# A decoder layer on one core: when the next sequence's first block may start, for the first two sequences

## The chip, the core and the metric

One of the eight cores of a Trainium2 chip runs the kernel. The metric is device time in microseconds (us), the median of several executions. All arrays are float32.

## What is computed

The layer takes 16 sequences of 512 tokens and 256 channels, and 64 context tokens of 128 channels for each. It has three blocks, and after each comes a layer norm of the input plus the block's result:

```python
x = layernorm(x + attn(x))      # gated long convolution, output projection, gated MLP
x = layernorm(x + xattn(x, ctx))
x = layernorm(x + ffn(x))       # low-rank: x@U1@V1 + b1, gelu, @U2@V2 + b2

# attn: z = rmsnorm(u)@in_proj.T, short causal conv, split in x2, x1, v
y   = (long_conv(x1*v) + x1*v*D_skip) * x2        # 16 poles per channel
y   = y@out_proj.T + u
mlp = gelu(zm@l1.T) * (zm@l2.T) @ l3.T            # zm = rmsnorm(y), 672 wide
return y + mlp

# xattn, 16 heads of 16:
y = softmax(causal(q@k.T))@v + softmax(qc@kc.T)@vc
return y@Wp + bp
```

Sequences are independent of each other in all of it.

## The kernel before

The kernel has two parts, each with a plan of its own. The front part goes over all 16 sequences and writes the long convolution (`yconv`) and the gates (`gates`) to DRAM. The second part, from line 990 on, goes through the sequences one after the other: `first_block(b)` (gate, output projection L1148, RMS norm, MLP L1173 to L1225, layer norm), `attention(b)` and `ffn(b)`. The change is in the second part.

The order of the work is not that of the code. Each step is recorded with `plan.op(engines, cost, fn, prio, ...)`. Dependencies come from the buffers that a step reads and writes (`r`, `w`) and from `after`. `Plan.schedule` (line 103) then plays the steps through with the given costs: at each moment a free engine takes, of the steps whose dependencies are done and whose buffers can be had, the one with the lowest priority number. On PE, `change` (line 95) adds a penalty or a bonus for leaving or keeping a tiling of the array. The result is one fixed order of instructions on each engine, in which each engine then runs on the chip. Priorities are built from the sequence: 1000 for each, so `first_block` of sequence b has (b-2)*1000+300, its MLP (b-1)*1000+100, attention's projections (b-1)*1000+600, its scores b*1000 and more.

Buffers are few. In PSUM `scores` is one buffer of four banks, `av` one bank, `mm` three banks. In SBUF there are one each of `yt` (the convolution's output of the current sequence), `gate`, `y1` and `gT`, three `xT`, five `xt`, six `row`, two `kcs` and two `ctx2`. `yt`, `gate` and one `xt` are the front part's `early` tiles; all other tiles of the second part lie where tiles of the front part lay, and their first writer waits until those are done with. `kcs` lies over front rows 3 and 4, `ctx2` over front row 5, and the last gates are stored from these rows (L541, L535).

The steps that matter here, by line:

- L1113, L1119, L1122: SP loads `yt`, `gate` and `xt` of a sequence. L1135: `yt` times `gate`, on DVE for sequence 0 and on POOL for the others.
- L1148: output projection, 8 instructions in two PSUM banks (`after=after`, line 1153). L1094: DVE adds it to the input and writes `y1`. L319, L308, L309, L1160, L335: RMS norm of `y1` on ACT and POOL. L348: transposes.
- L1173, L1185, L1190: five steps of the MLP, each four matmuls, a gelu on ACT and a product on DVE. L1203, L1211, L1216: its last 32 columns. L1225: the product with l3. L1046, L1047, L308 to L1055, L1067: layer norm.
- `attention`: L348 transposes the layer norm's output into `xT`; `begun` is the list of the steps that write it. L1254: values. L1278, L1286: context keys of two sequences into `kcs`. L1296, L1303, L299/L301: the context doubled by POOL into `ctx2`, and the context values. L1326, L1332: keys and queries; L1373, L1379: keys go through DRAM. L1388: context keys copied behind the keys.
- Maxima (L1421 to L1483): scores once, to find each row's maximum. For the first two and the last three sequences ACT copies the scores out (L1444), and POOL masks them (L1451). Sums (L1543, L1513, L1560, L1573): scores again, exponential on ACT, causal mask on POOL, product with the values; L1601 and L1621 are the same for the context. For sequences 0, 1 and 15 scores are written and copied in two halves.
- L1659 to L1708: the quotients, through DRAM. L1083: attention's output projection.

`begun` goes two ways. `attention(b)` uses it for `kc_mm` (line 1283) and for the doubled context (line 1299). It also returns it, and the loop at line 1815 hands it to `first_block(b + 1)`, whose output projection waits for it:

```python
    begun, held, kcs_of = (), [], []
    for b in range(B):
        x_ = first_block(b, begun)
        begun = attention(b, x_)
        ffn(b, x_)
```

Of the kernel before, what the change touches and what calls it, by code (L numbers as in the profile page):

```python
# [197 lines left out]
def decoder_layer(  # L198
# [141 lines left out]
    def transposed(src, view, prio, dst=None):  # L340

        dst = dst or Buf("xT")
        for k in range(KD):
            ps = Buf("mm")

            def tr(e, k=k, ps=ps):
                for c in range(NT):
                    nc.tensor.transpose(ps.t[:, bass.ts(c, P)], view(src.t)[:, c, bass.ts(k, P)], ident)  # L348

            plan.op("PE", TR, tr, prio, r=[src], w=[ps])  # L350
            plan.op(
                "ACT DVE", (act(T), dve(T)), lambda e, k=k, ps=ps: copy(e, dst.t[:, k, :], ps.t), prio,
                r=[ps], w=[(dst, k)],
            )
        return dst
# [16 lines left out]
    with ExitStack() as front:  # L372
# [69 lines left out]
        def as_xT(b):  # L442
            n = b - (B - KEPT)
            return View(f"e{n}" if 0 <= n < 3 else "x", lambda t: t.rearrange("p (k n) -> p k n", k=KD))

        def prepare(b, pr):

            x_ = View("x", lambda t: t.rearrange("p (c d) -> p c d", c=NT))
            for c in range(0, NT, 1 if b == 0 else NT):
                cs = slice(c, c + (1 if b == 0 else NT))  # L450
                plan.op(
                    "SP", 0.5 if b == 0 else 0.5 * MB,
                    lambda e, cs=cs: nc.sync.dma_start(
                        out=x_.t[:, cs, :], in_=x[b].rearrange("(c p) d -> p c d", p=P)[:, cs, :]
                    ),
                    pr - 1000, w=[(x_, c)] if b == 0 else [x_], lat=2.5, after=at_step(b - 3),
                )
            if b == 0:
                load_in(prew, pre_w, -900, [(INW, "p")])
                for k in range(KD):  # L460
                    load_in(inw[:, k, :], in_wT[bass.ts(k, P), :], -900, [(INW, k)])
                load_in(cw, conv_w, -890, [(CW, 0)])
                load_in(cb, conv_b, -890, [(CW, 1)])
                for k in range(KD):
                    plan.op(
                        "DVE", 0.9,
                        lambda e, k=k: nc.vector.tensor_scalar(
                            inw[:, k, :], inw[:, k, :], prew[:, k : k + 1], None, ALU.mult
                        ),
                        -900, r=[(INW, "p")], w=[(INW, k)],  # L470
                    )

            sq = rms_ops(x_, pr - 120)
            scale_ops(x_, sq, pr - 120, "POOL" if b else "DVE")
            xT = transposed(x_, lambda t: t, pr - 120, as_xT(b))
            marks.append(plan.ops[-1])
            return xT
# [69 lines left out]
        for b in range(B):  # L547
            xT = prepare(b, b * 100)
# [4 lines left out]
            else:  # L553
                if b < B - KEPT:
                    plan.op(
                        "SP", 0.5 * MB,
                        lambda e, b=b, xT=xT: nc.sync.dma_start(
                            out=normed[b - B + LATE], in_=xT.t.rearrange("p k n -> p (k n)")
                        ),
# [3 lines left out]
        for b, xT in late:  # L563
            if b < B - KEPT:
                xT = as_xT(b)
                plan.op(
                    "SP", 0.5 * MB,
                    lambda e, b=b, xT=xT: nc.sync.dma_start(
                        out=xT.t.rearrange("p k n -> p (k n)"), in_=normed[b - B + LATE]
                    ),  # L570
# [85 lines left out]
        for blk in range(NR // R8):  # L656
# [106 lines left out]
            for c in range(HPG):  # L763
# [8 lines left out]
                for par in range(2):  # L772
# [9 lines left out]
                    o = plan.op("ACT" if par and blk >= NR // R8 - 3 else "SP", 0.6, store, pc + 10, r=[res], lat=3.0)  # L782
# [318 lines left out]
    def add_row(x, row, prio):  # L1101
        def fn(e):
            nc.gpsimd.tensor_tensor(x.t, x.t, row.unsqueeze(1).to_broadcast([P, NT, D]), ALU.add)

        plan.op("POOL", pool_(NT * D), fn, prio, w=[x])
# [131 lines left out]
    def attention(b, x_):  # L1237

        p0, p1, p3 = (b - 1) * 1000 + 600, b * 1000, (b + 1) * 1000 + 250
        xT = transposed(x_, lambda t: t, p0)  # L1240
        begun = [o for _, o, w in xT.seen if w]
        add_row(x_, bias_p, p0 + 100)
        va, vc, yT = Buf("va"), Buf("vc"), Buf("xT")
        keys = [Buf("keys") for _ in range(G)]
# [569 lines left out]
# [5 lines that stand above are left out]
# [98 lines left out]
```

## Time and profile before

| | us |
|---|---|
| three runs | 2084.34, 2086.71, 2374.48 |
| median | 2086.71 |
| profiled execution | 2084.24 |
| its span, first to last instruction | 2082.2 |
| PE busy in the span | 2006.2 (96%) |
| DVE busy | 1329.4 (64%) |
| ACT busy | 1029.3 (49%) |
| POOL busy | 766.9 (37%) |

Busy times are sums over instructions of one engine. In timeline rows "xN" counts records of a line that follow each other; a float32 matmul leaves two records, so an L1148 of 8 instructions shows as x16. A bracket at the end of a row gives how long the engine had been idle and what ended that. The granted clock is the share of full speed that TensorE was given, and it is the mean over a stretch.

In this trace the front part's last matmuls end at 276, sequence 0's output projection begins at 281.56, its first MLP matmul starts at 297.81, its keys' projection at 335.98, its maxima at 358.24 and its sums at 400.06. Sequence 1's maxima start at 452.97, sequence 2's at 555.15.

### The profile page before, as it was taken

The numbers are of one execution on the slowest core, as the hardware profiler recorded it, in microseconds if no ns is written. First come the engines' busy times: TensorE is split into PE (matmuls) and PEld (weight loads), VectorE is DVE, ScalarE is ACT, GpSimd is POOL, SyncE is SP. The second block draws the span as 40 slices with busy tenths as digits, with TensorE's granted clock in tenths as the row PEclk, the third lists the DMA queues.
The fourth block names the chain that finished last, engine by engine and source line by source line (L and its number), as shares of the span: only waits on it lengthen the run. The fifth ranks groups of instructions, "written<-read, shape, count | busy, mean of one in ns | idle before, by whom it ended". The sixth has DMA issues, their size and how long they took to land. (4 is left out here: it accounts for less than half of the span.)

```text
span 2082.2 us, 36835 instructions
## 1 busy us (share of the span) xinstructions
PE 2006.2 (96%) x14900; PEld 1053.5 (51%) x14900; DVE 1329.4 (64%) x1920; ACT 1029.3 (49%) x1465; POOL 766.9 (37%) x1036
## 2 busy tenths in 40 slices
PE   7999978999999999999999999999999999999987
PEld 4455645555554545454545454454545454545443
DVE  7987533737584848484857576666767584656554
ACT  6864422656435262717161626253534446655773
POOL 7695612243323241414142424232323233533432
PEclk9999989999999999999999999999999999999999
DMA  6365861030304040413131312223131404031200
GB/s 195 110 212 184 273 214 51 6 119 17 119 11 144 12 134 22 123 33 117 38 108 48 100 56 88 68 70 85 56 100 33 123 13 129 18 101 45 71 22 31
DMA packets 114939, 182.22 MB, mean 88 GB/s; under 512 B 13393, under 2 KB 62034, under 8 KB 114642
## 3 DMA queue, kind: packets, MB, share of 16 engines
q1 hardware_dynamic: 113234, 177.26, 27.8%
q8 instruction: 117, 1.92, 0.4%
q10 hardware_dynamic: 1536, 2.62, 0.4%
q14 instruction: 52, 0.43, 0.1%
HBM read 111.09 MB, written 68.76 MB: 86 GB/s over the span
## 5 line engine op out<-in xcount | busy, mean ns | idle before, releaser
L1513 ACT ACTIVATE ex<-scores 128x2048 f32<-128x2048 f32 (+1 forms) x228 | 362.4, 1606 | 193.5 <-PE scores L1543 140.6
L1173 PE MATMUL mm<-xT,w_l 128*128 128x512 f32 x640 | 299.7, 609 | 0.0
L1560 POOL TENSOR_SCALAR_AFFINE_SELECT ex<-ex 128x512 f32<-128x512 f32 x256 | 158.6, 634 | 324.7 <-ACT ex L1513 323.2
L1421 PE MATMUL scores<-keys,q 32*128 32x192 f32 (+5 forms) x2848 | 225.3, 426 | 6.2 <-ACT ex L1444 4.6
L1543 PE MATMUL scores<-q,keys 32*128 32x256 f32 (+3 forms) x2240 | 183.3, 435 | 11.8 <-ACT ex L1513 10.9
L1421 PEld LDWEIGHTS scores<-keys,q 32*128 32x128 f32 x2848 | 123.8, 184 | 138.5 <-issue 41.1
L1772 ACT ACTIVATE row<-mm,b_s 128x512 f32<-128x512 f32 x124 | 78.9, 686 | 224.7 <-PE mm L1764 224.0
L1173 PEld LDWEIGHTS mm<-xT,w_l 128*128 128x128 f32 x640 | 114.6, 190 | 141.5 <-issue 134.3
L1703 POOL TENSOR_TENSOR nd<-nd,nd 128x1024 f32<-128x1024 f32 x30 | 70.7, 2357 | 299.9 <-DMA nd<-di 299.9
L1573 PE MATMUL av<-ex,va 128*32 128x512 f32 (+3 forms) x2048 | 164.8, 438 | 0.8 <-POOL ex L1560 0.8
L1225 PE MATMUL mm<-w_l,gT 128*128 128x256 f32 x640 | 160.7, 386 | 0.0
L308 POOL TENSOR_SCALAR small<-small 128x4 f32<-128x4 f32 (+1 forms) x66 | 13.2, 200 | 399.7 <-DVE small L1047 359.6
L500 DVE SCALAR_TENSOR_TENSOR frow<-fmm,cw,frow 128x511 f32<-128x511 f32 x192 | 141.0, 744 | 25.9 <-ACT frow L492 21.1
L1470 DVE TENSOR_TENSOR scores<-scores,mask_qk 128x1024 f32<-128x1024 f32 x132 | 115.6, 876 | 60.4 <-PE scores L1421 57.4
L1185 ACT ACTIVATE row<-mm 128x512 f32<-128x512 f32 x80 | 47.8, 598 | 209.6 <-PE mm L1173 209.6
L1543 PEld LDWEIGHTS scores<-q,keys 32*128 32x128 f32 x2240 | 96.9, 184 | 107.5 <-ACT ex L1513 67.3
L1444 ACT COPY ex<-scores 128x1024 f32<-128x1024 f32 (+1 forms) x96 | 114.3, 1228 | 65.7 <-PE scores L1421 53.0
L485 PE MATMUL fmm<-fx,inw 128*128 128x512 f32 x312 | 143.4, 604 | 0.0
L1225 PEld LDWEIGHTS mm<-w_l,gT 128*128 128x128 f32 x640 | 117.2, 190 | 44.6 <-issue 31.1
L299 DVE COPY row<-av 128x512 f32<-128x512 f32 x60 | 41.5, 691 | 134.9 <-PE av L1573 124.4
L1326 PE MATMUL mm<-xT,wqc_s 128*128 128x512 f32 x256 | 126.3, 611 | 0.0
L1332 DVE TENSOR_SCALAR q<-mm,bqc_s 128x512 f32<-128x512 f32 x62 | 46.6, 751 | 100.0 <-PE mm L1326 100.0
(210 smaller groups left out, 3485.9 us busy)
## 6 DMA issues: line engine op xcount, KB each, us to landing
dn<-row SPq DMA_DIRECT2D x120, 256.0 KB
keys<-dk SPq DMA_DIRECT2D x64, 256.0 KB
nd<-dn SPq DMA_DIRECT2D x30, 512.0 KB
nd<-di SPq DMA_DIRECT2D x30, 512.0 KB
fx<-hpad SPq DMA_DIRECT2D x28, 512.0 KB
early<-gates SPq DMA_DIRECT2D x16, 512.0 KB
early<-yconv SPq DMA_DIRECT2D x32, 256.0 KB
dk<-row SPq DMA_DIRECT2D x32, 256.0 KB
```

The source lines that it names most:

```text
L485: nc.tensor.matmul(ps.t, inw[:, k, bass.ts(m, P)], xT.t[:, k, :], start=(k == 0), stop=(k == KD - 1))
L500: lambda e, lag=lag: nc.vector.scalar_tensor_tensor(t.t[:, lag:], ps.t[:, 0 : T - lag], cw[:, m, 2 - lag : 3 - lag], t.t[:, lag:], ALU.mul ...
L1173: nc.tensor.matmul(ps.t, w[:, k, bass.ts(f, P)], zT.t[:, k, :], start=(k == 0), stop=(k == KD - 1))
L1225: nc.tensor.matmul(ps.t[:, bass.ts(cc, D)], gT.t[:, f, bass.ts(c, P)] if f < NF else gE.t, w_l3[:, f, :] if f < NF else w_l3e[:, c, :], st ...
L1326: nc.tensor.matmul(ps.t, w[:, k, cols], xT.t[:, k, :], start=(k == 0), stop=(k == KD - 1))
L1421: nc.tensor.matmul(sc.t[:, r, lo:hi], q.t[hd, bass.ts(i, P)], kk.t[hd, k0 - at + lo : k0 - at + hi], start=True, stop=True,)
L1444: lambda e, sc=sc, both=both, cols=cols: nc.scalar.copy(both.t[:, :, cols], sc.t[:, :, cols]),
L1470: nc.vector.tensor_tensor(diag, diag, mask, ALU.add)
L1513: lambda e: nc.scalar.activation(ex.t.rearrange("p (r n) -> p r n", r=HPG)[:, :, cols], sc.t[:, :, cols], AF.Exp, scale=scale),
L1543: nc.tensor.matmul(sc.t[:, r, lo:hi], keys[g].t[hd, TC + j * P : TC + (j + 1) * P], qas[g].t[hd, q0 + lo : q0 + hi], start=True, stop=True,)
L1560: lambda e, ex=ex, at=at: nc.gpsimd.affine_select(out=ex.t.rearrange("p (r n) -> p r n", r=HPG)[:, :, at : at + P], in_=ex.t.rearrange("p ...
L1573: nc.tensor.matmul(av[g].t[bass.ts(r, SLOT), j * P :], va.t[:, j, h * VS : h * VS + SLOT], ex.t[:, r * T + at : r * T + at + n], start=(j ...
```

## The change

For sequences 0 and 1 `begun` becomes an empty list. So the output projection of sequences 1 and 2 no longer waits for the previous sequence's transposes, and neither do the context keys of sequences 0 and 1 (computed once, with sequence 0) nor the doubled context of both. From sequence 2 on everything is recorded as before. What is computed is the same.

```diff
         p0, p1, p3 = (b - 1) * 1000 + 600, b * 1000, (b + 1) * 1000 + 250
         xT = transposed(x_, lambda t: t, p0)
-        begun = [o for _, o, w in xT.seen if w]
+
+        begun = [o for _, o, w in xT.seen if w] if b > 1 else []
         add_row(x_, bias_p, p0 + 100)
```

Lines after 1241 have a number one higher in the changed kernel. Costs, priorities and buffers stay as they are, and the plan is made anew from them.

## The prediction

> **What bounds the kernel now.** I read four things in this order: the page, the busy time by stretch, TensorE's timeline where the stretches show a gap, and ScalarE's timeline where a gap repeats. Times are us from the start of the span.
>
> The page gives PE 96% of the span. The stretches show where the other 4% lie. The scheduler starts afresh at 277, after the front part; the columns below are length, then busy time of PE, PEld, DVE, ACT, POOL with counts, granted clock, DMA share and GB/s.
>
> ```profile
> 284.30:298.00 13.70, 8.21 (x21) 5.48 (x22) 4.11 (x6) 3.93 (x13) 6.14 (x6) 0.62 0.73 250
> ...
> 328.70:334.20 5.50, 0.66 (x2) 0.28 (x2) 1.80 (x5) 1.61 (x4) 1.65 (x4) 0.99 0.00 0
> 334.20:346.00 11.80, 11.76 (x38) 8.04 (x39) 3.52 (x5) 3.10 (x10) 3.49 (x4) 0.72 0.16 46
> ...
> 358.20:400.00 41.80, 40.59 (x359) 23.73 (x358) 32.49 (x35) 26.50 (x32) 9.49 (x16) 1.00 0.01 4
> 400.00:437.40 37.40, 33.26 (x403) 19.15 (x402) 12.72 (x21) 26.63 (x34) 14.90 (x26) 1.00 0.17 56
> 437.40:453.00 15.60, 15.60 (x95) 8.23 (x94) 6.48 (x9) 5.16 (x12) 10.07 (x9) 1.00 0.55 142
> 453.00:499.20 46.20, 44.13 (x386) 25.60 (x385) 35.26 (x38) 28.95 (x35) 13.12 (x18) 1.00 0.19 60
> 499.20:536.30 37.10, 36.77 (x407) 22.22 (x407) 17.00 (x32) 26.48 (x32) 15.73 (x27) 1.00 0.16 53
> 536.30:558.30 22.00, 22.00 (x186) 12.54 (x185) 10.85 (x16) 8.04 (x20) 11.11 (x14) 1.00 0.53 156
> 558.30:664.70 106.40, 105.02 (x726) 53.24 (x722) 70.17 (x101) 47.30 (x60) 29.97 (x42) 1.00 0.25 75
> ```
>
> Two stretches are starved, 284 to 298 and 329 to 334. In 334 to 346 PE is busy but at a granted clock of 0.72, which costs 11.8 x 0.28 = 3.3. The softmax stages of sequence 0 (358 to 437) idle 5.3 together. After that PE is full.
>
> ```profile
> 281.56 2.04 PE L1148 MATMUL mm<-outw,early 128*128 128x256 f32 x4 [5.19 <-DVE early L1135]
> 284.33 5.49 PE L1148 MATMUL mm<-outw,early 128*128 128x256 f32 x12 [0.72 <-DVE early L1135]
> 294.93 0.88 PE L348 MATMUL mm<-ident,y 128*128 128x128 f32 x2 [5.12 <-ACT y L335]
> ...
> 333.24 0.33 PE L348 MATMUL mm<-ident,early 128*128 128x128 f32 x1 [4.60 <-ACT early L1067]
> ...
> 337.84 5.13 PE L1148 MATMUL mm<-outw,early 128*128 128x256 f32 x16
> ```
>
> PE waits for the gate product, for the RMS norm (5.12) and for sequence 0's layer norm (4.60). Nothing else is allowed: sequence 1's output projection waits for `begun`, the transposes at 333.24. It runs at 337.84 (x16 records are 8 instructions).
>
> ```profile
> 404.77 1.94 ACT L1513 ACTIVATE ex<-scores 128x1024 f32<-128x1024 f32 x2 [1.56 <-issue]
> 407.97 1.94 ACT L1513 ACTIVATE ex<-scores 128x1024 f32<-128x1024 f32 x2 [1.27 <-PE scores L1543]
> 411.24 1.94 ACT L1513 ACTIVATE ex<-scores 128x1024 f32<-128x1024 f32 x2 [1.33 <-PE scores L1543]
> ```
>
> A third limit: one scores buffer, so scores and exponential alternate and a fill comes every 3.27, however little else PE has to do. The copies of the maxima stage do the same at 3.30 (PE L1421 at 489.16 and 492.47, idle 1.42). With 12 fills each, such a stage lasts about 37 to 42, and PE is full in it only if some 2 us of other work stand between fills. That other work is what the change moves earlier.
>
> **The change part by part.** It empties `begun` for sequences 0 and 1. By the built order, sequence 1's projection and first two MLP steps move ahead of attention 0, sequence 2's projection moves ahead of attention 0's sums, and the context work of both moves to the very start. From the fourth sequence's value projection on (665 in this trace) PE's order is the same to the end, and so is that of DVE, ACT, POOL and SP from about there. So the time changes only by how much later or earlier that point is reached. I follow the delay against before; sequence 0 is the first.
>
> Start. Before, the first half of projection 0 (281.56, 2.04 long) hid in the wait for the second gate product. Now PE has L1278 and two L1303 ahead of it, DVE the key add L1286 and two context copies ahead of both L1135, and POOL two L1296 copies and five L1388 ahead of the first norm. The L1296 tile lies over a front row whose gate store (issued 277.3) lands at 282.7 by the trace's landing records. Then 0.29 copy, 0.3 to 0.6 matmul, 0.27 and 0.30 copies, again 0.30 for the second, hops of about 0.1: the first gate product starts at 284.85, ends 285.55, and the 2.04 half projection ends 287.6, against 284.33: +3.3. Bounds: below, the store lands with the others at 281.3, 1.4 earlier: +1.9; above, it takes as long as the ACT-issued store of 285.0, which landed at 291.9 (6.9 against 5.4): +4.8. I take the row of the store itself.
>
> RMS gap: stays, 5.1. What could fill it, two instructions of projection 1, stands behind the transposes and needs POOL's L1135, itself behind L1160. Moved work 2 x 0.43 and 0.2 wait: +1.1.
>
> MLP 0: 18.47 as before. One of three PSUM banks is now held by projection 1, but a step of four 0.86 instructions covers gelu (0.60) and product (0.69) with two.
>
> Rest of projection 1: 6 x 0.43 = 2.6, and since both halves and then L1203 use one bank, two evacuations stand bare (L1094 0.69 and hops, 0.95 each): +4.5. Behind L1203 the gelu L1211 queues on ACT after four L319 squares: +0.4. Layer norm 0 now begins 9.3 late.
>
> Layer norm gap: before, 7.34 from the last L1225 to the first key projection (328.64 to 335.98), idle and half clock. Now transposes of sequence 1 (1.04), MLP 1's first eight L1173 (6.9), three L1148 (1.3), own transposes (1.04) and 0.3: 10.6. Delay +12.6. Four idle us and the slow clock are gone, bought with work due later anyway.
>
> Projections 0: before 22.26 (335.98 to 358.24) with projection 1, its transposes, L1278, L1303 and the slow clock; now 12 x 0.86 + 8 x 0.43 + 0.43 + 0.4 = 14.5. Delay +4.8.
>
> Attention 0: maxima 41.8, now 42.0 by fills of at least 3.3 (filler 23.8 for 24.2). Sums 37.3, now 37.6: the 3.27 rhythm holds, and filler shrinks, so PE idles there instead. Delay +5.3. Projections 1: 15.6 before; of these, seven key and query instructions (6.0) and sequence 2's transposes (1.0) are now in the sums, while 2.7 of L1254 and L1203 come in: 11.1. Delay +0.8.
>
> Attention 1: maxima 46.2, PE full with 20 L1173; now less L1225 filler, 43.2 by fills, with two fills bare. Delay -2.2. Sums 37.1 at the rhythm both times. Then the bill: projection 3 (3.4), transposes (1.0) and one L1083 (0.4), filler in the sums before, now stand alone behind them: 26.4 for 22.0. Delay +2.2 at 558.
>
> From 558 to 665: same work, idle 1.4 before, about as much now. After: nothing. The sum is **+2.2**: 3.3 of slow clock and 4.9 of gap are won, 3.3 lost at the start, 2.3 in bare evacuations and the queued gelu, and some 5 as idle PE inside rhythms that have lost filler.
>
> SP: the gate load of sequence 3 now stands ahead of the first key stores; it waits for POOL's L1135 at about 336, the stores for keys of about 350, so it holds up nothing. The loads of sequence 3 stand ahead of the first L1659 stores and hold them some 7 us; what those feed (L1703, L1083) is due 70 us later. Nothing there.
>
> The profiled execution is 2084.24 (span 2082.2 and 2.0 around it); the three runs are 2084.34, 2086.71 and 2374.48, median 2086.71, so the profile lies 2.5 under it. 2084.24 + 2.2 = 2086.4, and I give 2087 between that and the median plus 2.2.
>
> [...] For the slow clock the row comes first: 0.72 over 11.8 us after a 4.6 gap, 3.3 lost. [...]
>
> **The rivals.** Faster: the rhythm does not bind and the won 3.3 + 4.9 stay. For it: in 453 to 499 PE was 96% busy, and 20 L1173 remain as filler there. Against it: 400 to 437 already idled 4.1 with more filler. With the start at its lower bound, the gain is 8.2 - 1.9 - 2.3 = 4, and 12 if the evacuations also hide and sums idle no more than before: 2072 to 2080.
>
> Slower: the start. The L1296 copy waits for a store in the densest traffic of the trace (250 to 283 GB/s in 276 to 298), and now three gate stores leave earlier and join it. Each us of landing is a us of delay, since no slack lies between it and attention 0. A landing after 287 decides: +4.3 on the sum, over the forecast's own range. With the longest wait on a gate store in this stretch (13.7, ACT L301) in place of the 5.4, it is 8.3 more, +10.5: 2091 to 2098.
>
> No effect: the y1, gate and product buffers are single, so sequence 2's part may not move usefully. Its projection does move by the order, but its MLP does not, and its price is inside the sum: 2084 to 2087.
>
> **How the numbers follow.** Forecast 0.50, own range 2081 to 2092 (+2.2 with start bounds -1.4 and +1.5, and 3 for the idle inside the rhythms); no effect 0.10; faster 0.18; slower 0.20; more than that 0.02. The range 2074 to 2100 leaves out the outer part of the faster case and the last. All cases lie within 42 us, 2%, which is about what a measurement of this kernel can tell from no change: faster 0.01, same 0.95, slower 0.04.
>
> **What would show it.** Right: first projection near 286 to 288; no PE gap over 1 us between 300 and 360 except about 0.95 twice around L1203; no layer norm gap; granted clock 1.00 from 305 on; maxima 0 from about 363; exponentials still 3.27 apart in both sums, with more PE idle in 400 to 440 and bare fills near 490; the point at 665 within 5 of 667. Wrong: the first projection after 292, ACT fills more than 3.5 apart, or a gap over 3 in sums 0 because sequence 1's layer norm is late on DVE behind the maxima.

## The result, and the profile after

| | median us | range | runs |
|---|---|---|---|
| before | 2085.19 | 2081.52 to 2374.48 | 22 |
| changed | 2090.28 | 2085.69 to 2094.30 | 22 |

The ratio is 1.0022, 95% interval 1.0016 to 1.0029: 4.6 us slower (3.3 to 6.0). A second measurement on another occasion gave 1.0019 (1.0010 to 1.0027), 4.0 us. The 2374.48 is one execution of before in a slow state, and the ratios leave it out. The forecast was 2087, with 2081 to 2092 as the likeliest case's own range, and no change that 2% can tell. That holds, and so does the sign of the small difference; its size is twice the +2.2 of the sum. The profiled execution took 2092.57, 2.3 above the median, and has a span of 2090.8.

Line numbers after 1241 are one higher. The stretches of the changed kernel, cut at the same events as those of before, with the same columns (length, busy time of PE, PEld, DVE, ACT, POOL with counts, granted clock, DMA share, GB/s):

```profile
338.90:349.10 10.20, 10.20 (x41) 5.88 (x39) 3.18 (x7) 4.93 (x9) 1.64 (x4) 1.00 0.15 51
349.10:363.30 14.20, 14.20 (x44) 7.78 (x42) 6.58 (x9) 1.02 (x4) 2.36 (x1) 1.00 0.30 80
363.40:404.80 41.40, 40.21 (x377) 26.37 (x376) 32.94 (x36) 24.97 (x29) 9.34 (x16) 1.00 0.03 11
404.80:444.00 39.20, 33.84 (x386) 16.65 (x386) 14.94 (x23) 27.87 (x37) 21.07 (x31) 0.96 0.32 97
444.00:454.90 10.90, 10.90 (x111) 6.77 (x110) 3.84 (x6) 3.50 (x4) 1.28 (x2) 1.00 0.32 97
454.90:498.00 43.10, 38.31 (x337) 21.27 (x336) 33.73 (x35) 26.69 (x31) 15.64 (x20) 0.99 0.17 52
498.00:536.30 38.30, 37.76 (x406) 21.39 (x406) 13.78 (x25) 24.05 (x27) 11.68 (x21) 0.92 0.15 51
536.30:564.60 28.30, 27.38 (x196) 16.64 (x196) 13.99 (x22) 13.53 (x28) 15.52 (x20) 1.00 0.45 139
564.60:671.60 107.00, 105.87 (x723) 53.72 (x722) 68.13 (x98) 46.68 (x59) 29.97 (x42) 1.00 0.24 70
```

Read the granted clock first. The layer norm gap and the slow clock behind it are gone (338.9 to 363.3: no idle time, 1.00). In their place the clock is 0.96 in sums 0 and 0.92 in sums 1, where before had 1.00. Busy time times the missing share of the clock gives what that costs: 33.84 x 0.04 = 1.4, 38.31 x 0.01 = 0.4, 37.76 x 0.08 = 3.0, together 4.8. TensorE also stands idle longer in maxima 1 (43.10 - 38.31 = 4.8, before 2.1) and sums 0 (5.4, before 4.1).

TensorE's timeline of the start and of projection 1:

```profile
285.57 2.08 PE L1304 MATMUL mm<-wcv_s,ctx 128*128 128x256 f32 x4 [5.63 <-POOL ctx L1297]
289.06 5.22 PE L1148 MATMUL mm<-outw,early 128*128 128x256 f32 x16 [1.41 <-DVE early L1135]
299.40 0.87 PE L348 MATMUL mm<-ident,y 128*128 128x128 f32 x2 [5.12 <-ACT y L335]
...
328.18 1.99 PE L1148 MATMUL mm<-outw,early 128*128 128x256 f32 x8 [0.84 <-DVE y L1094]
331.02 1.08 PE L1203 MATMUL mm<-xT,w_l 128*32 128x128 f32 x32 [0.85 <-DVE y L1094]
```

Projection 0 now stands behind the context products and ends at 294.3 instead of 289.8. The RMS wait stays at 5.12, and the two bare evacuations show as 0.84 and 0.85.

Where the clock is lost, in TensorE's timeline of sums 0 and of the turn from maxima 1 to sums 1:

```profile
404.78 1.15 PE L1544 MATMUL scores<-q,keys 32*128 32x256 f32 x16 [0.55 <-ACT ex L1445]
408.03 1.99 PE L1544 MATMUL scores<-q,keys 32*128 32x256 f32 x24 [2.10 <-ACT ex L1514]
409.95 1.86 PE L1574 MATMUL av<-ex,va 128*32 128x512 f32 x8
...
412.33 1.15 PE L1544 MATMUL scores<-q,keys 32*128 32x256 f32 x16
...
494.77 1.15 PE L1422 MATMUL scores<-keys,q 32*128 32x256 f32 x16 [2.09 <-ACT ex L1445]
497.96 2.09 PE L1544 MATMUL scores<-q,keys 32*128 32x256 f32 x16 [2.05 <-ACT ex L1445]
...
503.69 1.17 PE L1544 MATMUL scores<-q,keys 32*128 32x256 f32 x24
```

The x16 of scores takes 1.15 at 404.78 and 2.09 at 497.96; the instructions are the same. Ahead of the slow one TensorE waited twice for ScalarE's copies, 2.09 and 2.05, with 1.15 of work between. So one fill takes 5.73 (497.96 to 503.69) and another 4.30 (408.03 to 412.33), where the rhythm was 3.27. ScalarE shows the same from its side, exponentials 4.07 apart and then 3.49:

```profile
406.04 1.94 ACT L1514 ACTIVATE ex<-scores 128x1024 f32<-128x1024 f32 x2
410.11 1.94 ACT L1514 ACTIVATE ex<-scores 128x1024 f32<-128x1024 f32 x2 [2.14 <-issue]
...
413.60 1.94 ACT L1514 ACTIVATE ex<-scores 128x1024 f32<-128x1024 f32 x2 [1.15 <-PE scores L1544]
```

### The profile page after: what moved, and what is told of

It reads as the page before. It is cut to its first block, busy times and chain, and to the rows that moved or that the text cites. A ratio compares the mean times of both kernels' runs of the same rounds, so it can differ in the third digit from the quotient of the medians.

```text
span 2090.8 us, 36836 instructions
## 1 busy us (share of the span) xinstructions
PE 2008.6 (96%) x14900; PEld 1055.3 (50%) x14900; DVE 1327.8 (64%) x1918; ACT 1031.1 (49%) x1467; POOL 767.6 (37%) x1036
```

## The experiments

Two measures go with each run. "Time" is the ratio to the kernel before on the same chip less one, times 2085, with its 95% interval. "Stretch" is read in the profiled execution, from sequence 0's first MLP transposes (L348 on `y`; its time in the span is "begin") to sequence 3's first maxima, from where all kernels have the same work. So begin holds the start, stretch all the rest of the change.

| kernel | time, us | begin | stretch |
|---|---|---|---|
| before, two profiles | 0 | 294.93, 297.35 | 369.74, 369.76 |
| changed, first | +4.6 (3.3 to 6.0) | 299.40 | 372.16 |
| changed, again | +4.0 (2.1 to 5.6) | 298.54 | 370.65 |
| projections only | +2.3 (0 to 4.6) | 291.42 | 372.87 |
| context only | -1.0 (-3.1 to 1.0) | 297.96 | 367.88 |
| second sequence only | +4.2 (1.9 to 6.5) | 295.40 | 371.67 |
| changed, waits filled with two | 0.0 (-2.3 to 2.5) | 299.87 | 367.20 |
| changed, waits filled with one | +0.8 (-1.3 to 2.9) | 296.50 | 366.76 |
| changed, first of two waits filled | +4.6 (2.7 to 6.3) | 297.65 | 370.84 |
| changed, RMS wait filled too | +0.4 (-1.5 to 2.3) | 303.06 | 366.02 |
| projections only, filled | +0.4 (-1.5 to 2.3) | 293.14 | 369.83 |
| before, norm gap filled | +0.6 (-1.3 to 2.3) | 293.53 | 371.32 |
| before, both gaps filled | -0.6 (-2.5 to 1.3) | 298.54 | 369.72 |

### Which part costs

Projections only: `attention` keeps `begun` for itself and returns an empty list for sequences 0 and 1.

```diff
-        begun = [o for _, o, w in xT.seen if w] if b > 1 else []
+        begun = [o for _, o, w in xT.seen if w]
...
-        return begun
+        return begun if b > 1 else []
```

> Only the output projections of sequences 1 and 2 are set free; context keys and doubled context wait as before. Differences are against the kernel before, which the changed kernel exceeds by 4.6 us. My theory: the change loses in three places that its trace shows, the start (1.8 us net of the front part's later end), sums 0 (1.9), and from maxima 1 to the point where both orders meet again (216.2 us against 211.2, 5.0); it wins the layer norm gap and the slow clock. Here the 1.8 at the start goes, but 1 to 2 us of context products (L1279 1.05, two L1304 of about 0.5) come back among the projections: +3.5 to +5.0, first projection where before has it, and maxima 1 to the meeting point again about 216. Rival S, the start's wait for the context copy is the whole loss: 0 to +1.

Measured +2.3 (0 to 4.6), between the two. From maxima 1 to maxima 3 it takes 215.7, as the changed kernel (216.7) and not as before (211.7). It lacks one loss, in sums 0:

```profile
402.31 1.16 PE L1544 MATMUL scores<-q,keys 32*128 32x256 f32 x24 [2.10 <-ACT ex L1514]
...
491.66 2.09 PE L1544 MATMUL scores<-q,keys 32*128 32x256 f32 x16 [2.05 <-ACT ex L1445]
```

The first row has the same 2.10 of waiting before it as the row at 408.03 above, and yet full clock, 1.16 for x24 against 1.99 (the end of "Is it the clock?" compares the two); the second is as slow as in the changed kernel.

Context only: the other half.

```diff
-        begun = [o for _, o, w in xT.seen if w] if b > 1 else []
+        shown = [o for _, o, w in xT.seen if w]
+        begun = shown if b > 1 else []
...
-        return begun
+        return shown
```

> Only the context keys and the doubled context of sequences 0 and 1 are set free; the projections wait as before, and from the first third of that stage on the order is that of before. My theory: +1.8 us at the start as in the changed kernel, given back by 2 us of context products that no longer stand among the projections of 0 and 1: -0.5 to +1.0 against before, layer norm gap (4.6) and sums 0 (37.3) as before. Rival S, the start is the whole loss: +1.8 to +4.6. A third view, that nothing but the moved second stage matters: 0.

Measured -1.0 (-3.1 to 1.0), stretch 1.9 shorter than before: the 2 us of context products are gone from it as my theory said. The start alone is not the loss.

Second sequence only: `if b != 1` in place of `if b > 1`.

> Only sequence 1 gives an empty list, so sequence 2's projection is free and all of sequence 1's waits as before; from maxima 1 on TensorE's order is that of the changed kernel. My theory: start, layer norm gap and maxima 0 as before; sums 0 take in more work, so maxima 1 begin 2 to 4 us earlier than before; then the changed kernel's 216 instead of 211 us to the meeting point, with two bare fills at the end of maxima 1 and the first sums 1 at half clock (2.09 for x16): +1 to +3.5 against before. Rival S, the start is the loss: -3 to 0. Rival R, that the loss sits in the stage of sequence 0 and its delayed layer norm alone: -3 to 0 as well, with the second stage at 211.

Measured +4.2 (1.9 to 6.5), above what I expected. The stretch has what I expected: maxima 1 begin 92.7 after maxima 0 (before 94.7), then 215.9 instead of 211.7 to maxima 3. Both rivals fall, since they had no loss here. The second stage loses by itself, with the layer norm gap of before still in place. Only 1.9 of the 4.2 lies in the stretch; the other 2.3 would be the start, where part of the context work has moved, and this run doesn't separate it.

### Is it the clock?

Waits filled with two: the changed kernel with six products that nobody reads, in the same order otherwise. (Each such line in these kernels adds 2 to line numbers behind it.)

```diff
                             at += k1 - k0
+                        for _ in range(2 if b == 1 and g == 3 and use[0][0] != 1 and cols.stop == T else 0):
+                            nc.tensor.matmul(pool["av"][0][:, 0:D], ident, outw[:, 0, :], start=True, stop=True)
...
                             at += T - j * P
+                        for _ in range(2 if b == 0 and g0 == 0 and uses == fills[0] and cols.stop == T else 0):
+                            nc.tensor.matmul(pool["av"][0][:, 0:D], ident, outw[:, 0, :], start=True, stop=True)
```

> The changed kernel with six added products of 128x256 that nobody reads, written to the free av bank: two behind the first scores of sums 0 and two behind each of the last two scores of maxima 1, where TensorE stands idle for about 2 us. All else is in the same order. My theory: after those idles the granted clock is half (2.09 us for the first x16 of sums 1, 1.99 for x24 of the second fill of sums 0, 1.86 for x8 of av), and that makes fills of 4.68 and 5.73 out of 3.3 to 3.4. With the waits filled (about 0.9 of 2.1 us each) these rows go to about 1.15, 1.26 and 1.06 and the fills to 3.3 to 4.3: 2 to 3.5 us faster than the changed kernel, +1 to +2.6 against before. Rival: the fills are long because of what ScalarE waits for, and the clock is no cause: as the changed kernel, or up to 1 us slower.

Measured 0.0 (-2.3 to 2.5): work was added and some 4 us were won. Its windows over sums 0 and sums 1, and its first scores of sums 1:

```profile
405.40:443.60 38.20, 33.37 (x396) 16.70 (x396) 14.94 (x23) 27.86 (x37) 21.09 (x31) 1.00 0.33 99
...
497.50:533.30 35.80, 35.11 (x402) 19.90 (x402) 13.79 (x25) 24.05 (x27) 11.70 (x20) 1.00 0.16 55
```

```profile
497.52 1.15 PE L1546 MATMUL scores<-q,keys 32*128 32x256 f32 x16 [0.99 <-ACT ex L1447]
```

Clock 1.00 in both, sums 1 in 35.8 instead of 38.3, sums 0 in 38.2 instead of 39.2. The first fill of sums 1 takes 3.25 in place of 5.73 (the next scores start at 500.77). ScalarE's and VectorE's busy times are unchanged to 0.01, so nothing else became faster. The rival, that ScalarE alone sets these fills, falls.

First of two waits filled: two products behind the last scores but one of maxima 1 only.

> The changed kernel with two added products in the first of the two 2.1 us waits at the end of maxima 1; the second wait and sums 0 are left as they are. If the half clock needs both waits (idle 2.1, busy 1.15, idle 2.05), the first x16 of sums 1 goes from 2.09 to about 1.15 and sums 1 shorten by 2 to 3 us: +1.5 to +2.5 against before. If the second wait alone is enough, these rows stay at 2.09 and 1.22 and the time is the changed kernel's, +4.6.

Measured +4.6 (2.7 to 6.3), nothing won:

```profile
493.13 1.15 PE L1422 MATMUL scores<-keys,q 32*128 32x256 f32 x16 [1.03 <-ACT ex L1447]
496.32 2.09 PE L1546 MATMUL scores<-q,keys 32*128 32x256 f32 x16 [2.05 <-ACT ex L1447]
```

Filling one of the two was not enough: behind the 1.03 left of the first wait, 1.15 of work and the second wait of 2.05 the x16 still took 2.09.

Filled with one: one product in place of two in each of the three waits.

> The changed kernel with one product instead of two in each of the three waits (two in maxima 1, one in sums 0): TensorE is then busy about 1.7 of 3.3 us in them, against 1.15 unfilled and 2.3 with two. With two, the rows behind were at full clock (1.15 for x16), without at half (2.09). If half busy is enough to hold the clock: 1.15 and +0 to +1 against before. If not: 2.09 and +3.5 to +5.

Measured +0.8 (-1.3 to 2.9). In the changed kernel's trace the clock goes to 0.50 at 496.93, 1.03 ahead of the first scores of sums 1, and back at 503.76, 6.83 us later, two steps of 3.41 (on these steps see below). Cut in such steps, first the changed kernel and then this one, whose cut lies 1.21 ahead of its first scores:

```profile
493.52:496.93 3.41, 1.15 (x16) 0.72 (x16) 2.37 (x3) 2.15 (x4) 0.63 (x1) 1.00 0.00 0
496.93:500.35 3.42, 2.39 (x17) 1.59 (x18) 2.58 (x3) 2.49 (x4) 0.64 (x1) 0.50 0.00 0
500.35:503.76 3.41, 3.41 (x12) 2.22 (x11) 0.58 (x1) 1.71 (x2) 0.64 (x1) 0.50 0.00 0
```

```profile
488.22:491.64 3.42, 1.77 (x18) 1.02 (x18) 2.39 (x3) 2.15 (x3) 0.63 (x1) 1.00 0.00 0
491.64:495.05 3.41, 2.20 (x21) 1.75 (x22) 2.57 (x3) 3.38 (x5) 0.63 (x1) 1.00 0.00 0
```

Busy 1.15 of 3.41 (34%) was followed by 6.8 us at 0.50, busy 1.77 (52%) by a step at 1.00. The work of the two differs by a single product of 0.6.

Changed again: the same kernel, for a second profile.

> The changed kernel once more, for a second profile of it. Theory: +3.3 to +6 against before as measured; the first scores of sums 1 at about 2.1 us again, since both waits there add to 4.1; the second fill of sums 0 at half clock or not, as chance has it (the same waits left it at full clock in the projections-only trace); from the RMS wait to maxima 3 between 370.5 and 372.5. If the half clock of the first trace was a chance of that execution: first scores of sums 1 at 1.15 and the stretch at 369 or less.

Measured +4.0 (2.1 to 5.6). Both places are at half clock again, so the loss isn't a chance of one execution:

```profile
407.19 1.97 PE L1544 MATMUL scores<-q,keys 32*128 32x256 f32 x24 [2.10 <-ACT ex L1514]
...
497.13 2.09 PE L1544 MATMUL scores<-q,keys 32*128 32x256 f32 x16 [2.05 <-ACT ex L1445]
```

Why does a wait of 2.1 us in sums 0 cost clock here and not in the projections-only trace? In the traces of before and of the changed kernel the granted clock is either 1.00 or 0.50, and within each of the two all its changes lie whole multiples of 3.41 us apart: in the changed kernel's, 408.19 to 411.60 is one such step, 411.60 to 496.93 is 25 and 496.93 to 503.76 two. Here are the steps around that wait, first in the changed kernel, then with projections only:

```profile
404.77:408.19 3.42, 1.31 (x20) 0.89 (x24) 2.70 (x3) 3.19 (x3) 1.70 (x3) 1.00 0.56 158
408.19:411.60 3.41, 3.41 (x32) 1.63 (x32) 1.67 (x6) 1.49 (x2) 1.20 (x2) 0.50 0.00 0
```

```profile
397.61:401.03 3.42, 2.05 (x21) 1.17 (x19) 2.50 (x4) 3.39 (x4) 0.63 (x1) 1.00 0.49 143
401.03:404.44 3.41, 2.12 (x33) 1.15 (x33) 3.08 (x8) 2.08 (x3) 1.87 (x2) 1.00 0.06 15
404.44:407.85 3.41, 2.76 (x40) 1.52 (x36) 2.73 (x4) 2.48 (x6) 2.51 (x4) 1.00 0.00 0
```

In the changed kernel the wait (405.93 to 408.03) lies whole in one step, which holds 1.31 of work (38%), and the next step is at half clock. With projections only the border at 401.03 splits it (400.21 to 402.31), both steps hold 60% or more, and the clock stays. So what sets the two apart is TensorE's work within a step. A count over the traces of before and of the changed kernel, from 340 us to the end, says the same: five steps at full clock had at most 41% of work (0 to 1.39 us), and a step at half clock came after each; 1,010 had 48% or more, and none came after those. Ahead of 340 the two traces don't divide so cleanly: the clock held after 1.40 (before, from 327.24) and 1.47 (changed, from 278.48) and fell after 1.42 (before, from 122.44). Half clock lasted longer than one step where the step at half clock was itself not full: over both traces all six such steps with 79% of work or less were followed by another one, and of the 15 with 90% or more only one was (before, from 334.07, 95%). The one from 496.93 was 70% busy, and the loss in sums 1 lasted two steps; the one from 408.19 was full, and in sums 0 it lasted one. This also suggests why the turn to sums 1 lost in all three traces shown above in which both its waits were bare (2.09 at 497.96, 497.13 and 491.66): with the 1.15 of work between them they span 5.3 us, and wherever the borders fall, some step is left with at most about 1.4 of work (an estimate from the rows at 494.77 and 497.96).

### Can the older waits be filled too?

Before with the layer norm gap filled: eight products ahead of sequence 0's transposes, in `transposed`.

```diff
             def tr(e, k=k, ps=ps):
+                for _ in range(0 if k else warm):
+                    nc.tensor.matmul(ps.t[:, 0:D], ident, outw[:, 0, :], start=True, stop=True)
                 for c in range(NT):
```

> The kernel before with eight added products of 128x256 (0.43 us each, 3.4 in all) that nobody reads, in the 4.6 us gap ahead of sequence 0's transposes; all else in the same order. Theory H, the idle time costs twice, once itself and once as a low granted clock behind it: the key and query projections behind the gap (11.8 us at 0.72) get the full clock and end about 3 us earlier: -3.3 to -2 against before. Theory I, the clock is low there for another reason than the gap, or the added products delay the transposes: 0 to +1.

Measured +0.6 (-1.3 to 2.3): a miss. The clock fell all the same, later:

```profile
328.37:331.78 3.41, 3.41 (x17) 2.83 (x15) 1.79 (x5) 0.00 (x0) 1.10 (x2) 1.00 0.00 0
331.78:335.20 3.42, 1.79 (x9) 0.94 (x8) 0.26 (x1) 2.07 (x4) 0.55 (x3) 1.00 0.00 0
335.20:338.61 3.41, 3.07 (x7) 1.72 (x6) 0.43 (x1) 0.58 (x1) 2.57 (x2) 0.50 0.00 0
```

By the numbers alone the run is with theory I. The eight products ran at the head of the gap, up to 332.0, and so filled the step before the one that counted. That one, from 331.78, held 1.79 (52%), nearly all of it transposes that each waited for a row of the norm, and half clock followed; with one product in each wait the clock held after a step of 1.77, also 52%. So the run doesn't refute that the gap lowers the clock, and doesn't show it either. A further 1.4 was lost in sums 0, at a clock of 0.96.

Before with both gaps filled: six more products in the RMS wait, in the same way.

> As the run with the layer norm gap filled, with six more such products (2.6 us at full clock) in the 5.1 us wait for sequence 0's RMS norm. In the trace of before 5.15 us of busy time are lost to the slow clock from that wait to maxima 0, some 3.3 behind the layer norm gap, the rest behind the RMS wait. Theory H: -5 to -3.5 against before, granted clock near 1.00 from the first MLP matmuls on. Theory I: 0, or +1 to +3 if the six run at half clock and outlast the wait.

Measured -0.6 (-2.5 to 1.3), the same miss: the six products ended 2.32 us ahead of the transposes, and the first MLP matmuls ran at 0.51. The step in the norm gap held 1.96 of 3.42 (57%), part of it transposes, and half clock followed again.

Changed with the RMS wait filled too: six products there, and two in each of the three waits.

> The changed kernel with the six products in sequence 0's RMS wait, two behind the first scores of sums 0 and two behind each of the last two scores of maxima 1. With nearly all slow clock gone (3.06 us from the RMS wait to maxima 0, 4.75 in sums 0, maxima 1 and sums 1 of the changed kernel's trace), what is left of the change is its start and its idle time: the stretch from the RMS wait to maxima 3 comes to about 365, against 372.2 in the changed kernel, and the time to -3.5 to -2 against before, but 2 to 3 above the kernel before with both gaps filled. If the start is all that the change costs, it would be 4 to 5 above that kernel.

The stretch came to 366.0 as expected (365), the time to +0.4 (-1.5 to 2.3), 2 to 4 more than expected, with the latest begin of all profiles (303.06): a miss. It stands 1.0 above before with both gaps filled, which is less than the two intervals can tell.

Projections only, filled: that kernel with two products behind the last two scores of maxima 1, and six in the RMS wait.

> Projections of sequences 1 and 2 free, context held as before, six products nobody reads in sequence 0's RMS wait and two behind each of the last two scores of maxima 1. Theory: the start is that of before, the clock loss of the projections-only trace (0.77 in maxima 1, 2.24 in sums 1, some 1.2 behind the RMS wait) goes, so the stretch from the RMS wait to maxima 3 comes to 368 to 369 instead of 372.9 (before 369.7): 0 to -2 against before. If the start is no part of the changed kernel's loss: as the changed kernel with all filled, about +0.4.

Measured +0.4 (-1.5 to 2.3), stretch 369.8 against 372.9 unfilled: the loss in sums 1 is gone, that behind the RMS wait is not (the clock from there to maxima 0 is 0.95 in both). The time is the one named for the case that the start is no part of the loss, but the interval takes in both cases, so the run doesn't settle what the start costs.

Before again, for a second profile of its start.

> The kernel before once more, for a second profile of its start. In the four traces without context work at the start, sequence 0's first MLP transposes begin at 291.4 to 298.5 from the start of the span (mean 294.6), in the six with it at 295.4 to 303.1 (mean 298.9). Theory: the start costs about 3.3, so again 291 to 299 here. If the first trace of before began early by chance: over 299.

It began at 297.35, as the theory has it. Its sums 0 differ from those of the first profile, where 400.00:437.40 had 1.00:

```profile
401.10:439.80 38.70, 34.66 (x401) 19.76 (x400) 12.72 (x21) 26.54 (x34) 14.88 (x26) 0.96 0.16 54
```

34.66 x 0.04 = 1.4 lost in one execution of the same kernel and not in the other. Here too the place of the step's border differs: the wait of 2.06 lies whole in a step with 1.36 of work (422.22 to 425.64) in the second profile, and in the first the border at 422.81 splits it into steps with 2.17 and 2.22. So a single wait of this length went one way in one execution and the other way in the next, and the fair comparison for the 39.2 of the changed kernel is 37.4 to 38.7.

No version is faster than the kernel before by more than the intervals; the lowest are context only (ratio 0.9995, 0.9985 to 1.0005) and before with both gaps filled (0.9997, 0.9988 to 1.0006).

## Why the prediction was right, and where it was wrong

**Start, +3.3 predicted.** The first profiles of both kernels differ by 4.5 (projection 0 ends at 294.3 and 289.8). The begin column scatters by about 7 us among kernels with the same start, so single profiles don't decide. Its mean is 299.0 over the seven traces with the whole context work at the start and 294.8 over the six with none: 4.2. The timed runs give less: time minus the stretch's difference from before is on average 2.9 for the six such kernels (the changed one with the means of its two measurements) and -0.5 for the four others, 3.4 apart. The run with the second sequence only, left out here since it moves only part of the context work, gives 2.3. Context only speaks for a smaller price (-1.0 + 1.9 = 0.9, at most 2.9 by its interval). So the predicted size fits, and its exact value stays open. The first projection came at 289.06 and 288.15, a little behind the 286 to 288 named. The chain was the one predicted: the copy of the context waits for the store of gates. The profile names that store in the second trace, while the first names the key add, which ended as the copy began and had itself waited for a store of gates:

```profile
285.23 0.53 POOL L1297 COPY ctx<-ctxT 128x128 f32<-128x128 f32 x2 [14.41 <-DVE kcs L1287]
```

```profile
284.32 0.53 POOL L1297 COPY ctx<-ctxT 128x128 f32<-128x128 f32 x2 [14.81 <-DMA gates<-frow]
```

A landing after 287, from which the slower rival was to decide, didn't come in these two; in the trace with the RMS wait filled too the copy came at 287.6, and that trace has the latest begin, 303.06.

**RMS gap, MLP 0, projection 1, layer norm gap.** From begin to maxima 0: 64.0 in both traces, before 63.3 and 61.9; predicted was +1.5 (4.8 - 3.3), measured +0.7 and +2.1. The wait stayed at 5.12, the evacuations stood bare, the layer norm gap closed. The sign I had named, a granted clock of 1.00 from 305 on, held in the stretches up to sums 0 and not after.

**Projections 1 and maxima 1.** 10.9 for 11.1 predicted, 43.1 for 43.2, with two bare fills near 490 as forecast. Maxima 0 took 41.4 for 42.0.

**Sums 0 and 1: the step that failed.** The prediction had "Sums 37.1 at the rhythm both times" and, for sums 0, "37.6: the 3.27 rhythm holds, and filler shrinks, so PE idles there instead". They took 39.2 and 38.3. It had priced an idle TensorE in a bare fill at the idle time itself, covered by ScalarE's rhythm. That idle time had a second price here: after steps with 38% and 34% of work the clock was 0.50, for 3.4 us in sums 0 and 6.8 in sums 1, and TensorE, with 1.99 for x24 of scores and 1.86 for x8 of av, became what the next exponential waited for (1.15 at 413.60). I had seen this only behind the 4.6 us gap. One of the signs named for being wrong appeared with it: exponentials more than 3.5 apart (4.07). The second price explains the sign of the result: with the three waits filled, the time is that of before (0.0, +0.8, +0.4), without, +4.0 to +4.6. So the forecast held in part by luck: the sum lacked about 4 us of slow clock, and without that loss the change costs less than its +2.2, by about 2, which is as much as these intervals can tell. The two errors partly cancel.

**Behind sums 1.** 26.4 predicted, 28.3 in the first trace, where the transposes of sequence 3 waited 0.5 for their norm, and 26.8 in the second. Then 107.0 for 106.4, predicted equal. The stretch's sum was -1.1 by the prediction, and +2.4 and +0.9 in the traces.

**The rivals.** Faster: it asked for the 8.2 of gap and slow clock to stay won. The gap and the clock behind it were won, and the start and the fills with their slow clock took it back. No effect: refuted by +4.6 (3.3 to 6.0).

**The slow clock.** Ahead of sums 1 of the changed kernel half clock came after a step of 3.41 us that held 1.15 of work (from 493.52), with no wait over 2.1, and the same wait falls differently on the steps from one profile to the next. Behind the norm gap of before half clock lasted two steps (334.07 to 340.89), which held 6.65 of work: at 0.50 that is the 3.3 of the row. The two norm gap runs stay open: steps of theirs with 52% and 57% of work, nearly all or partly transposes, were followed by half clock, while with projections only a step of the front part with 1.64 of transposes in a row (48%, 97.24 to 100.65) kept the clock. A transpose alone shows as 0.33 (before, 333.24), and in such a row, 16 records in 1.91 (before, 97.41), as 0.12, so the busy time in the gap may simply overstate the work; no run here tests this.

## What to carry to other kernels

Work that is pulled forward is taken from somewhere: look for the waits it used to fill, and price each not only by its idle time but by the clock of what follows, which here cost an estimated 4.8 us from sums 0 to sums 1 (the windows of the changed kernel). In a timeline, the sign was one instruction shape with two durations, 1.15 and 2.09, behind waits of about 2 us. A single wait of 2.1 cost clock where it lay whole in one step of 3.41 us (1.31 of work) and none where a border split it (2.05 and 2.12), so one profile without the loss doesn't show that there is none. Compare single profiles only stretch by stretch: the start alone scattered by about 7 us, more than the 4.6 the change cost.

## What the runs showed of the hardware that was not expected

In the traces of before and of the changed kernel the granted clock was 1.00 or 0.50, and changed only at multiples of 3.41 us that run through the whole trace. From 340 us on, the five steps with at most 41% of work were each followed by half clock, and the 1,010 with 48% or more were not. None of the waits behind the loss in sums 1 was as long as a step: two of 2.1 us with 1.15 of work between them were followed by 6.8 us at 0.50, and with 0.6 us of added products within the step the clock stayed at 1.00. Filling the head of a longer wait did not help: with eight products at the head of the norm gap, up to 332.0, the clock was 0.50 from 335.20 to 338.61 (before: from 334.07 to 340.89).
